# SBUF tiles that take their buffers from lists, in a two-layer graph transformer on one core

## The chip, the core and the metric

The kernel runs on one core of a Trainium2 chip. The core has TensorE (PE, matrix products into PSUM), VectorE (DVE), ScalarE (ACT), GpSimd (POOL) and SyncE (SP); DMAs move data between HBM and the on-chip memory SBUF, or within SBUF. The engines run side by side, each through its own instructions in a fixed order, and wait for each other by semaphores. The metric is the device time of one execution in microseconds (us), the median of several runs.

## What is computed

32 graphs of 512 nodes with 256 features, each with its own 512 x 512 adjacency matrix, go through two layers; a residual and a layer norm close each of them. Cut to what matters:

```python
# layer 0
allowed = (adj > 0) | (adj.T > 0) | eye
q, k, v = split(x @ Wqkv.T + bqkv)               # 8 heads of 32
attn = softmax(where(allowed, q @ k.T / sqrt(32), -inf))
h = layernorm(x + (attn @ v) @ Wo.T + bo) * g1 + b1_
h = layernorm(h + relu(h @ W1.T + b1) @ W2.T + b2) * g2 + b2_
x = layernorm(x + h)
# layer 1: attention alone, with the mask adj != 0
x = layernorm(x + attention(x, adj) @ Wo.T + bo)
```

Everything is in float32 but the masks, which are bfloat16.

## The kernel before

A class `Graph` holds the tiles of one graph and one small method for each step. Of a layer's attention, the part that matters here works on chunks of 128 keys x 4 heads x 512 queries; a layer has 8 of them, k = 0 to 7, of which 0 to 3 belong to the first four heads. For chunk k of a layer:

- `scores` (L404): 8 products on TensorE in narrow tiles write s, which takes 4 of the 8 PSUM banks. There is only one s, so the next `scores` waits until `exp` has read it.
- `exp` (L413): ScalarE writes p = exp(scale * s), 128 x 2048 float32, 1.88 us.
- `masked` (L417): VectorE multiplies p by the mask in place.
- `product` (L424): TensorE multiplies p with v into acc.
- For the softmax's sums, the four p of a head group are added up. `pair(layer, k)` (L437) is a DMA issued by GpSimd that adds p(k + 1) into p(k) within SBUF, 1 MB; `fold` (L440) adds two p on VectorE; `halve` (L464) adds one half of a p's partitions into the other by a DMA, and `spread` (L469) takes four pieces of it to a tile `part`. Where the sums aren't spread, `sums` (L448) adds over the keys with a product by ones.

So some p are last read by TensorE or VectorE, and others (1 and 5 of each layer, above all) by a DMA that lands some microseconds after it is issued.

The order of all this is written out by hand: `opening` for the first graphs (called with graphs 0 to 4 as a to e), `period` for the steady part (called 26 times; graphs k to k + 4 are at different stages of their way), `closing` for the last five (graphs 27 to 31 as a to e). The block runs under a manual schedule: each engine gets its instructions in the order in which the lines are written. A method only names its engine. `bias`, `masks`, `join` and the norms of five graphs thus lie between the products of others.

Tiles come from pools. `at(tag, n, shape)` asks a pool for a tile with a tag. The tag has a fixed number of buffers: 8 for p, 4 for y, r and st, 2 for z, v, kT and total. In the kernel before, the pool gives out one of these buffers by itself. The tile then waits for every user of the tile that had the buffer before: `exp` into a p waits until the old p's last reader is done, be it an engine or a DMA. PSUM banks for all products but s and acc don't go this way: `bank` takes the number of the bank from a string, `banks`, one digit for each tile in the order of asking, with a pattern repeated 13 times (for two calls of `period` each) between an opening and a closing part.

The places that the prediction speaks of, in the order of the code: in `opening`, graph 0's `pair(0, 4)` at L688 and graph 1's `exp(0, 3)` at L698; further down

```python
            a.exp(1, 5)          # L955
            ...
            a.exp(1, 6)          # L970
            ...
            a.pair(1, 4)         # L1013
            ...
            c.scores(0, 2)       # L1026
            c.exp(0, 2)          # L1027
            ...
            c.scores(0, 1)       # L1034
            ...
            c.exp(0, 5)          # L1041
```

and in `closing` `b.pair(1, 4)` (L1898), `d.exp(0, 1)` (L1922) and `d.exp(0, 4)` (L1935).

Of the kernel before, what the change touches and what calls it, by code (L numbers as in the profile page):

```python
# [9 lines left out]
F32 = mybir.dt.float32  # L10
# [17 lines left out]
def kernel(ctx: ExitStack, tc: tile.TileContext, t: dict, out: bass.AP):  # L28
# [14 lines left out]
    B, N, D = x.shape  # L43
    P = 128
    NQ = N // P
# [19 lines left out]
    total = const.tile([P, N // HD], F32, name="total")  # L65
# [85 lines left out]
    def plain(pools: ExitStack):  # L151
# [4 lines left out]
        ps_d = pools.enter_context(tc.tile_pool(name="ps_d", bufs=3, space=PSUM))  # L156
        hbm = pools.enter_context(tc.tile_pool(name="hbm", bufs=2, space=bass.MemoryType.DRAM))

        def dense(out, lhsT, rhs, start, stop, wide):
# [3 lines left out]

        SPREAD = {(0, 0), (1, 0)}

        banks = iter(
            "012012021021122121012012010210210210201012102021121021012012012012102102102102102020120122021201212101120120212010"
            + "120121212010121212012012120120021212102101010212101010210210102102201010" * 13
            + "102120201210021021010210102102102021201021010210202101201201210210212102102102121021021021021021202102120120"
        )  # L170

        SMALL = {"y", "z", "cent", "sT", "total", "r", "st", "part"} | {
            f"{t}{n}" for t in ("mv", "rs", "ms") for n in range(1, 5)
# [2 lines left out]
        class Graph:  # L176
# [6 lines left out]
            def at(self, tag, n, shape, dtype=F32, **kw):  # L183

                key = (tag, n)
                if key not in self.tiles:
                    name = f"{tag}_{self.b}" + "".join(f"_{i}" for i in (n if isinstance(n, tuple) else () if n is None else (n,)))
                    pool = small if tag in SMALL else ps_s if tag == "s" else ps_a if tag == "acc" else work
                    self.tiles[key] = pool.tile([P, *shape], dtype, tag=tag, name=name, **kw)
                return self.tiles[key]  # L190

            def bank(self, kind, n, shape):

                key = (kind, n)
                if key not in self.tiles:
                    name = f"ps{kind}_{self.b}" + "".join(f"_{i}" for i in n)
                    self.tiles[key] = ps_d.tile([P, *shape], F32, tag=f"d{next(banks)}", name=name, bufs=1)
                return self.tiles[key]

            def final(self, layer):  # L200

                return self.b == B - 1 and layer == 1


            @property
# [191 lines left out]
            def scores(self, layer, k):  # L397
                hg, kc = divmod(k, NQ)
                s = self.at("s", (layer, k), [HPC, N])
                for j in range(HPC):  # L400
                    at = slice(j * HD, (j + 1) * HD)
                    for half in range(2):
                        key = kc * P + half * P // 2
                        nc.tensor.matmul(  # L404
                            s[half * P // 2 : (half + 1) * P // 2, j, :],
                            self.kT(layer)[at, hg, key : key + P // 2],
                            self.qT(layer)[at, hg, :],
                            start=True,
                            stop=True,
                        )  # L410
# [31 lines left out]
            def sums(self, layer, hg):  # L442

                ps = self.bank("R", (layer, hg), [N])
                folded = [2 + hg] if not self.final(layer) else range(hg * NQ, (hg + 1) * NQ)
                for k in folded:
                    for j in range(HPC):
                        nc.tensor.matmul(  # L448
                            ps[j * HD : (j + 1) * HD, :],
                            ones,  # L450
                            self.p(layer, k)[:, j, :],
                            start=(k == folded[0]),
                            stop=(k == folded[-1]),
                        )


            def spread_out(self, layer, hg):

                return (layer, hg) in SPREAD and not self.final(layer)

            def halve(self, layer, hg, rows):

# [2235 lines left out]
    with ExitStack() as pools:  # L2698
        plain(pools)
# [207 lines left out]
```

## Time and profile before

| | |
|---|---|
| time before, median of 3 runs | 3014.59 us (3012.68 to 3015.29) |
| the profiled execution's own time | 3012.29 us |
| its span, first to last instruction | 3010.5 us |
| granted TensorE clock, mean | 0.995 |
| `exp` L413, ACT | 512 times, 1881 ns each, 963.0 us busy |
| `masked` L417, DVE | 512 times, 2278 ns each, 1162.5 us busy |
| `fold` L440, DVE | 189 times, 2281 ns each, 431.0 us busy |
| `pair` L437, DMA | 189 times, 1024 KB, 7.9 us from issue to landing (median) |
| share of DMA engines in use | 0.6 to 0.7 in most slices |

A row of busy times gives an engine, its busy time, its share of the span and its number of instructions. In the slices, each digit is the busy share of a fortieth of the span in tenths. A line of the list of waits says who waited, at which line, for what, and then the total in us, the number of times and the longest. A line of the timeline has start, length, engine, line, operation, tile written and tiles read; in brackets it has the idle time of the engine before it and what ended it. A line of the stretches has the stretch, its length, the busy time of PE, PEld, DVE, ACT and POOL with the number of instructions, the granted clock (1.00 is full), the share of the DMA engines and GB/s. The idle time of an engine that nobody waits for costs nothing.

### The profile page before, as it was taken

Reading aid. Unit: us, or ns where it says so; the run is one execution under the profiler, and the core shown is the slowest. Engines: PE = TensorE matmul, PEld = TensorE weight load, DVE = VectorE, ACT = ScalarE, POOL = GpSimd, SP = SyncE. Lnnn points to the kernel's source line nnn. Section 1 sums busy time; section 2 is a strip of 40 time slices with the busy share of each in tenths; the row PEclk is TensorE's granted clock in tenths of the full one; section 3 lists DMA queues with packets and bytes.
Section 4 is the critical chain, followed back from the end, with each engine's and each line's share of the span. In section 5 each row is a group of like instructions: output and inputs, shape, how many; then the busy total and the mean of one; then the engine's idle time right before and its main releaser. Section 6 shows DMA issues by size and latency. Waiting matters only on the chain.

```text
span 3010.5 us, 82999 instructions
## 1 busy us (share of the span) xinstructions
PE 2959.1 (98%) x36442; PEld 1375.9 (46%) x36442; DVE 2707.0 (90%) x3588; ACT 1746.2 (58%) x2111; POOL 972.2 (32%) x1252
## 2 busy tenths in 40 slices
PE   7989999999999999999999999999999999999997
PEld 2544445544444444445444445444454444454443
DVE  4879999999999999999999999999999999998996
ACT  4446655566565566565566655665655665556654
POOL 0222433233333233333233332333332333323241
PEclk9999999999999999999999999999999999999999
DMA  7867767676666676676666666766666776767560
GB/s 157 137 118 134 140 130 138 128 144 126 135 136 126 129 146 134 131 137 125 137 135 135 132 132 127 147 127 132 134 130 130 145 132 128 137 127 136 102 113 27
DMA packets 277169, 391.22 MB, mean 130 GB/s; under 512 B 153376, under 2 KB 237472, under 8 KB 246048
## 3 DMA queue, kind: packets, MB, share of 16 engines
q0 software_dynamic: 36304, 264.53, 47.6%
q1 hardware_dynamic: 240496, 121.32, 18.4%
q8 instruction: 288, 4.72, 0.7%
q14 instruction: 81, 0.66, 0.1%
HBM read 72.23 MB, written 33.55 MB: 35 GB/s over the span
## 4 chain that ended last, share of the span: by engine, by line
PE 93%; DVE 3%; DMA 2%; ACT 1%; issue 1%; POOL 1%; SPq 0%; DVEq 0%; POOLq 0%; ACTq 0%
PE s L404 17%; PE psF L162 14%; PE acc L424 14%; PE psH L162 14%; PE psQK_None L162 11%; PE psV L162 7%; PE psO L162 7%; PE psQK L162 4%; PE psT L365 2%; PE psR L448 2%; DMA p<-p 1%; DVE p L417 1%; ACT p L413 1%; DVE p L440 1%; DMA w_L_gnn_Wqkv<-in_L_gnn_Wqkv_dram 0%
## 5 line engine op out<-in xcount | busy, mean ns | idle before, releaser
L413 ACT ACTIVATE p<-s 128x2048 f32<-128x2048 f32 x512 | 963.0, 1881 | 496.2 <-PE s L404 459.8
L417 DVE TENSOR_TENSOR p<-p,m 128x2048 f32<-128x2048 f32 x512 | 1162.5, 2278 | 49.9 <-ACT p L413 46.7
L404 PE MATMUL s<-qT,kT 32*64 32x512 f32 x8192 | 572.7, 615 | 22.7 <-ACT p L413 21.4
L424 PE MATMUL acc<-p,v 128*32 128x512 f32 x4096 | 507.7, 596 | 1.6 <-ACT cT L433 1.5
L162 PE MATMUL psH<-xT,w_L_gnn_W 128*32 128x256 f32 (+1 forms) x6200 | 471.2, 380 | 1.5 <-DVE bov L321 1.5
L162 PE MATMUL psF<-w_L_gnn_W,hT 128*32 128x256 f32 (+1 forms) x6704 | 459.9, 380 | 0.0
L440 DVE TENSOR_TENSOR p<-p,p 128x2048 f32<-128x2048 f32 x189 | 431.0, 2281 | 10.7 <-DMA p<-p 9.4
L539 POOL TENSOR_SCALAR rs<-mv 128x2 f32<-128x2 f32 (+1 forms) x320 | 196.5, 614 | 726.6 <-DVE mv L534 713.3
L162 PEld LDWEIGHTS psH<-xT,w_L_gnn_W 128*32 128x32 f32 (+1 forms) x6200 | 302.7, 119 | 199.1 <-issue 55.3
L540 POOL TENSOR_TENSOR rs<-rs,neg_half 128x2 f32<-128x2 f32 (+1 forms) x320 | 369.7, 1155 | 26.7
L162 PEld LDWEIGHTS psF<-w_L_gnn_W,hT 128*32 128x32 f32 (+1 forms) x6704 | 291.2, 116 | 178.8 <-ACT hT L575 32.6
L437 POOL DMA_DIRECT2D p<-p x189 | 174.1, 921 | 530.0 <-PE acc L424 460.4
L575 ACT ACTIVATE hT<-psH,c_L_gnn_b 128x256 f32<-128x256 f32 x512 | 211.4, 474 | 200.0 <-PE psH L162 200.0
L404 PEld LDWEIGHTS s<-qT,kT 32*64 32x64 f32 x8192 | 119.5, 130 | 335.4 <-issue 113.2
L464 POOL DMA_DIRECT2D p<-p x126 | 107.8, 855 | 464.5 <-DVE mv L534 196.2
L162 PE MATMUL psQK_None<-xT,w_L_gnn_Wqkv 128*32 128x512 f32 (+1 forms) x2012 | 246.5, 598 | 5.6 <-DMA w_L_gnn_Wqkv<-in_L_gnn_Wqkv_dram 4.7
L162 PE MATMUL psO<-w_L_gnn_Wo,cT 128*32 128x256 f32 (+1 forms) x2776 | 241.8, 381 | 1.8 <-DVE cT L510 1.8
L424 PEld LDWEIGHTS acc<-p,v 128*32 128x32 f32 x4096 | 119.7, 110 | 253.0 <-issue 187.9
L162 PEld LDWEIGHTS psO<-w_L_gnn_Wo,cT 128*32 128x32 f32 (+1 forms) x2776 | 155.3, 123 | 99.2 <-issue 45.6
L370 ACT COPY xT<-psT 128x512 f32<-128x512 f32 x130 | 76.0, 585 | 198.9 <-PE psT L365 198.8
L560 ACT ACTIVATE x<-z,ms,rs 128x256 f32<-128x256 f32 x128 | 73.2, 597 | 167.2 <-DVE ms L544 164.0
L531 DVE BATCH_NORM_STATS2 st<-y 128x6 f32<-128x256 f32 x384 | 155.0, 422 | 6.2
(77 smaller groups left out, 2845.3 us busy)
## 6 DMA issues: line engine op xcount, KB each, us to landing
p<-p POOLq DMA_DIRECT2D x189, 1024.0 KB, 7.9
p<-p POOLq DMA_DIRECT2D x63, 512.0 KB, 5.9
x<-in_x_dram SPq DMA_DIRECT2D x32, 512.0 KB, 4.2
code<-in_adj_dram POOLq DMA_DIRECT2D x32, 512.0 KB, 5.9
m<-code SPq DMA_DIRECT2D x32, 512.0 KB, 4.9
out_dram<-x SPq DMA_DIRECT2D x32, 512.0 KB, 6.2
p<-p POOLq DMA_DIRECT2D x63, 256.0 KB, 6.3
part<-p SPq DMA_DIRECT2D x252, 64.0 KB, 2.0
```

The costliest lines, as they stand in the source:

```text
L162: nc.tensor.matmul(out[at], lhsT[:, at], rhs, start=start, stop=stop)
L404: nc.tensor.matmul(s[half * P // 2 : (half + 1) * P // 2, j, :], self.kT(layer)[at, hg, key : key + P // 2], self.qT(layer)[at, hg, :], st ...
L413: nc.scalar.activation(self.p(layer, k), self.at("s", (layer, k), [HPC, N]), AF.Exp, scale=SCALE)
L417: nc.vector.tensor_tensor(p, p, m[:, k % NQ, None, :].to_broadcast([P, HPC, N]), ALU.mult)
L424: nc.tensor.matmul(acc[j * HD : (j + 1) * HD, :], self.v(layer)[:, kc, h * HD : (h + 1) * HD], self.p(layer, k)[:, j, :], start=(kc == 0), ...
L437: nc.gpsimd.dma_start(out=self.p(layer, k), in_=self.p(layer, k + 1), accum_op=ALU.add)
L440: nc.vector.tensor_tensor(self.p(layer, dst), self.p(layer, a), self.p(layer, b), ALU.add)
L464: nc.gpsimd.dma_start(out=p[:rows], in_=p[rows : 2 * rows], accum_op=ALU.add)
L531: nc.vector.bn_stats(self.at("st", (n, i), [6]), self.y(n, i))
L539: nc.gpsimd.tensor_scalar(rs, self.mv(n)[:, a:b, 1:2], EPS, None, ALU.add)
L540: nc.gpsimd.tensor_tensor(rs, rs, neg_half[:, a:b, None], ALU.pow)
L575: nc.scalar.activation(self.hT(h)[:, f, :], ps[:, f % 2, :], AF.Relu, bias=b1[:, f : f + 1])
```

## The change

Eight kinds of tile in SBUF (p, y, z, st, r, v, kT and total) take their buffer from a string of digits, as the PSUM banks did and do. In `at`, a tag found in `slots` is replaced by the tag with the next digit, with one buffer of its own. The number of buffers of each kind stays the same, and so does the order of the steps. `final` is renamed `direct`, with the same meaning.

```diff
-        banks = iter(
-            "012012021021122121012012010210210210201012102021121021012012012012102102102102102020120122021201212101120120212010"
...
-        )
+        slots = {
+            "d": iter(
+                "012012021021122121012012010210210210201012102021121021012012012012102102102102102020120122021201212101120120212010"
...
+            ),
+            "p": iter(
+                "012345673267415013405762302764517064153205732146706431520752136450436217051726431"
+                + "036472501257436206435710271536470436152075216435036421705172436106437250125736420436571027156437036415207521436506432170517236410436725012576432036457102715436706431520752136450436217051726431" * 2
+                + "03642750175246370435612072516437063124563452170"
+            ),
+            "y": iter(
+                "01231023012301231023100113201320232301321023020231201302"
+                + "303021031230232301321023020231201302" * 8
+                + "3202132031200210203102312020021032101230"
+            ),
+            "z": iter(
...
+            "st": iter(
...
+            "r": iter(
...
+            "v": iter(
+                "0110011"
+                + "0011" * 13
+                + "00110"
+            ),
+            "kT": iter(
...
+            "total": iter(
...
+        }
...
                     pool = small if tag in SMALL else ps_s if tag == "s" else ps_a if tag == "acc" else work
+                    if tag in slots:
+                        tag, kw = f"{tag}_{next(slots[tag])}", {"bufs": 1}
                     self.tiles[key] = pool.tile([P, *shape], dtype, tag=tag, name=name, **kw)
...
-                    self.tiles[key] = ps_d.tile([P, *shape], F32, tag=f"d{next(banks)}", name=name, bufs=1)
+                    self.tiles[key] = ps_d.tile([P, *shape], F32, tag=f"d_{next(slots['d'])}", name=name, bufs=1)
...
-            def final(self, layer):
-
-                return self.b == B - 1 and layer == 1
+            def direct(self, layer):
+
+                return (self.b, layer) == (B - 1, 1)
```

## The prediction

> **What bounds the kernel now.** I read four views in this order: the page's busy times, its slices, the list of TensorE's waits, and the timeline around the longest of those waits. First busy times and slices:
>
> ```profile
> PE 2959.1 (98%) x36442; PEld 1375.9 (46%) x36442; DVE 2707.0 (90%) x3588; ACT 1746.2 (58%) x2111; POOL 972.2 (32%) x1252
> PE   7989999999999999999999999999999999999997
> ```
>
> TensorE has 3010.5 - 2959.1 = 51.4 us without a matmul, and the slices put it at both ends: the middle is full. The steady part shows this best, cut into stretches of one repetition (91.58 us, PE busy next to it):
>
> ```profile
> 450.00:541.58 91.58, 91.58 (x1120) 43.02 (x1116) 84.71 (x113) 54.56 (x67) 30.85 (x39) 1.00 0.68 134
> 2000.00:2091.58 91.58, 91.58 (x1124) 43.03 (x1116) 84.71 (x113) 54.56 (x66) 31.29 (x39) 1.00 0.68 133
> ```
>
> There TensorE never waits, so no choice of buffers can shorten the 26 repetitions; it can only spoil them. A gain must come from the 51.4 us at the ends. What they wait for, in TensorE's own list of waits (us in total, times, longest):
>
> ```profile
> PE s L404 <- ACT p L413: 21.4, 19, 8.5
> PE psT L365 <- DMA x<-in_x_dram: 4.9, 1, 4.9
> ```
>
> and, from the view of line 413, what the exponentials themselves waited for (us, times):
>
> ```profile
>   PE s L404: 459.8, 349
>   DMA p<-p: 16.7, 3
> ```
>
> Three exponentials waited for a DMA that moves p into p. An exponential reads scores s and writes a fresh p; such a DMA gives it no data. It can only have been waiting for its buffer, which the DMA was still reading. The timeline shows the largest of the three, and below it the chain of waits gives the transfer's length:
>
> ```profile
> 178.91 1.11 PE L404 MATMUL s<-qT,kT 32*64 32x512 f32 x16
> 179.96 3.66 PE L162 MATMUL psF<-w_L_gnn_W,hT 128*32 128x256 f32 x64
> 180.65 1.08 POOL L437 DMA_DIRECT2D p<-p  x1
> 190.18 1.88 ACT L413 ACTIVATE p<-s 128x2048 f32<-128x2048 f32 x1 [11.34 <-DMA p<-p]
> 192.09 2.29 DVE L417 TENSOR_TENSOR p<-p,m 128x2048 f32<-128x2048 f32 x1 [8.54 <-ACT p L413]
> 192.11 2.02 PE L404 MATMUL s<-qT,kT 32*64 32x512 f32 x16 [8.49 <-ACT p L413]
> ...
> 180.65 9.45 DMA p<-p
> ```
>
> The scores end at 180.02; the exponential starts at 190.18, just after the transfer lands (180.65 + 9.45 = 190.10). All of s's PSUM is held meanwhile, so TensorE stops at 183.62, and VectorE with it. The two others are at 68.77 (1.05 us) and 2755.20 (4.29 us).
>
> **What the Trainium skill says.** "Perfetto Trace Analysis", Optimization Strategy, takes *consistent* bubbles on the engine that should be saturated as a hint that buffers are too few. Here the bubbles are three single ones and the repetitions have none, so the number of buffers (8) suffices, and which one is taken is what hurts. "TensorE: Matmul & The Clock Gate", What's actually happening, says that about 3.4 us of idling halves the clock until a busy window has passed. The trace agrees, in stretches with the granted clock third from the end:
>
> ```profile
> 188.00:192.00 4.00, 0.00 (x0) 0.00 (x0) 0.00 (x0) 1.82 (x2) 0.00 (x0) 0.56 0.92 183
> 192.00:194.00 2.00, 1.89 (x16) 0.33 (x16) 1.91 (x1) 0.53 (x2) 0.00 (x0) 0.50 0.69 103
> 194.00:196.00 2.00, 2.00 (x17) 1.83 (x10) 0.72 (x2) 1.78 (x2) 0.00 (x0) 0.68 0.45 93
> ```
>
> So the stall is paid once more after it ends. "DMA: Bandwidth & Descriptors", Anatomy of one DMA, fits a GpSimd-issued DMA as 2.0 us + bytes / 436e3, which for this 1,024 KB gives 4.4 us; here the median is 7.9 us and these two took 9.45 and 10.83, so I use the trace's.
>
> **The change, part by part.**
>
> *Order.* Built, both programs have the same instructions in the same order on all five engines. TensorE's and SyncE's waits are the same too. What differs is addresses and, on ACT, DVE and POOL, waits for a buffer's last users. Following each tile to the tile that had its buffer before it: 279 of 512 p and 54 of 384 y follow another tile; st, r, z, v, kT and totals follow the same one as before, so those lists change nothing. The rename of `final` changes nothing either.
>
> *Waits added.* For every wait that only the changed program has, I looked up the instruction that ends it and when that ended in the trace of before. The tightest, once in each repetition, is an exponential (at 368.94, 460.51, ... 2658.39) that takes a p whose fold on VectorE ended 2.84 us before. Next come 3.28 us (exponential at 2758.40) and 5 us and up; VectorE's tightest is 5.2 us, POOL's 18. None binds: 0 us. ACT gains 28 semaphore instructions, median 38 ns in the view of line 413, 1.1 us over the run on an engine idle 42% of the time: 0 as cost, bound 0 to 1.1.
>
> *Waits removed that did bind.* Only three exponentials in the program lose a wait that ended within 0.5 us of their start. They are the three above.
>
> (1) 190.18, `c.exp(0, 2)`: it held the buffer of p(1, 5) of graph 0, which `a.pair(1, 4)` reads. The list gives it that of p(1, 6), whose last user, a fold, ended at 177.94. It then waits for its scores alone, so it starts at 180.1 and ends at 182.0, before TensorE runs out at 183.62. The 8.49 us go. VectorE finished at 183.55, so its 8.54 us go too, and both engines continue in the same relation as before. The clock: from 192.11 the three groups s x16, psT x4, psF x16 took until 198.67 (6.56 us); the same three took from 2761.77 to 2766.77 at full clock (5.00 us). So 1.56 us come back, at most; the matmuls after it that wait for VectorE had 2.16 us and more to spare. (1) is 8.49 + 1.56 = 10.05, bounds 8.49 and 10.05.
>
> What is late next: the buffer under the DMA now goes to `c.exp(0, 5)`, which started at 199.89. Moved by 10.05 it would start at 189.84, and the transfer lands at 190.10: 0.3 us late. Behind it on ACT is a relu (203.49) that had 1.72 us of idling before it, so nothing passes on. SyncE's loads in 184 to 203 don't move with TensorE; the nearest consumer is the transpose of `part` at 207.10, landed at 194.46, 12.6 us to spare against 10.05.
>
> (2) 2755.20, `d.exp(0, 1)` in the closing:
>
> ```profile
> 2755.20 1.88 ACT L413 ACTIVATE p<-s 128x2048 f32<-128x2048 f32 x1 [4.29 <-DMA p<-p]
> 2757.14 1.12 PE L404 MATMUL s<-qT,kT 32*64 32x512 f32 x16 [2.51 <-ACT p L413]
> ...
> 2744.29 10.83 DMA p<-p
> ```
>
> Its scores ended at 2751.99; the new buffer's fold at 2748.85. It starts at 2752.1, ends at 2753.9, and TensorE goes on at 2754.63: 2.51 us. The buffer under the DMA (landing 2755.12) goes to `d.exp(0, 4)`, which moves from 2758.40 to 2755.89: still 0.7 us to spare. No halved clock here. Bounds 1.8 and 2.51.
>
> (3) 68.77: the exponential could start at 67.88, 0.9 us earlier. But VectorE's fold at 68.75 needs the same transfer's data, and later an edge mask's load, paced by SyncE's queue, ends a wait of all:
>
> ```profile
> 89.81 1.22 DVE L284 TENSOR_TENSOR m<-m,m 128x2048 bf16<-128x2048 bf16 x1 [3.20 <-DMA m<-code]
> 92.50 3.72 PE L162 MATMUL psH<-xT,w_L_gnn_W 128*128 128x256 f32 x16 [1.54 <-DVE bov L321]
> ```
>
> That load doesn't come earlier, so I take 0, bounds 0 and 0.9.
>
> **Sum.** 10.05 + 2.51 + 0 = 12.56 us. Span 3010.5 - 12.6 = 2997.9; the profiled execution took 3012.29, 1.8 around its span, hence 2999.7. The median shown is 2.3 us above that execution, so 3014.59 - 12.56 = 3002.0. Least: 8.49 + 1.8 - 1.1 = 9.2, 3005.4. Most: 10.05 + 2.51 + 0.9 = 13.5, 3001.1.
>
> **The rivals.** A measurement of this kernel can tell about 0.2%, 6 us, from no change; so faster means under 3008.6.
>
> *The wait only moves on.* The same transfer stalls `c.exp(0, 5)` instead. For it: 0.3 us late already. Against: 1.72 us of idle ACT behind it. The longest p<-p landing in the trace is 11.9 us, 2.45 more than this one; then 2.75 - 1.72 = 1.0 us is lost, and the clock's 1.56 as well: 3002.0 + 2.6 = 3004.6.
>
> *VectorE takes it back.* It is busy 84.7 of 91.58 us in a repetition, and the stall was also its rest. Were it behind by then, TensorE would wait for it within a repetition and the 8.49 return. For it: 90% busy. Against: it stood idle through the same stall, with nothing queued. Then 2.51 + 1.56 = 4.1 are left: 3010.5, no change.
>
> *A new wait in every repetition.* The exponential with 2.84 us to spare is the place. Every us by which VectorE's fold comes later than that costs 1 us in each of 26 repetitions. To end 6 us above 3014.59, 18.6 us beyond the gain, it takes 0.72 us each: the fold 3.6 us later than now. For it: 26 times the leverage. Against: the spare time is 2.84 or 2.85 in all of them, with nothing moved inside a repetition. At that point: 3021.
>
> *The lists choose what the pool chose.* So it is for six of the eight kinds. For p it is excluded by the 279.
>
> **How the numbers follow.** Both stalls go, 0.74, 3002.0; the wait moves on, 0.13, 3004.6; VectorE takes it back, 0.08, 3010.5; a new wait, 0.05, 3021. Faster 0.87, same 0.08, slower 0.05. Predicted 3002.0. Range 2998.5 to 3007: the sums above (3001.1 to 3005.4) with some 2 us for the spread of the runs shown (3012.68 to 3015.29), holding the first two cases.
>
> **What would show it.** Right: no exponential with a wait for DMA p<-p; TensorE's longest wait on ACT p far under 8.5 us; granted clock 1.00 from 180 to 200; 91.58 us in the middle as before; the psH after the bov wait still at 92.5. Wrong: a wait over 0.5 us at `c.exp(0, 5)`, TensorE waiting for DVE p before 300 us, a repetition longer than 91.6, or a new bubble in the closing.

## The result, and the profile after

Run in turns on the same chip, six times each, the changed kernel took 2999.16 us (2997.37 to 2999.72) and the kernel before 3012.35 us (3011.72 to 3015.29): a ratio of 0.995, interval 0.994 to 0.9961. The forecast was 3002.0, 2.8 us more. The gain between the medians is 13.2 us, against 12.56 summed, and the interval, some 12 to 18 us, holds both. But 12.56 had been taken off 3014.59, the median of the first three of these six runs of before, and the median of all six is 3012.35. The profiled execution of the changed kernel took 2999.72 us.

The page after, in its span, busy times and the slices of TensorE:

```profile
span 2998.0 us, 83024 instructions
PE 2959.6 (99%) x36442; PEld 1374.8 (46%) x36442; DVE 2707.0 (90%) x3588; ACT 1747.1 (58%) x2111; POOL 978.6 (33%) x1252
PE   7999999999999999999999999999999999999997
```

TensorE is busy for as long as before (2959.1), in a span that is 12.5 us shorter: 38.4 us without a matmul are left of 51.4. The second slice, which was an 8, is a 9. The middle is unchanged, in the same two stretches of one repetition (length, then busy time and instructions of PE, PEld, DVE, ACT and POOL, granted clock, DMA share, GB/s), as are the ones around the first stall, which is gone:

```profile
450.00:541.58 91.58, 91.58 (x1127) 42.94 (x1116) 84.74 (x113) 54.57 (x66) 30.94 (x40) 1.00 0.70 134
2000.00:2091.58 91.58, 91.58 (x1118) 42.93 (x1117) 84.71 (x113) 54.56 (x67) 31.15 (x39) 1.00 0.68 133
...
184.00:188.00 4.00, 4.00 (x33) 2.88 (x22) 3.39 (x3) 2.35 (x2) 0.00 (x0) 1.00 0.96 195
188.00:192.00 4.00, 4.00 (x45) 1.52 (x47) 4.00 (x5) 0.00 (x0) 0.00 (x0) 1.00 1.08 152
192.00:194.00 2.00, 2.00 (x44) 1.19 (x39) 1.08 (x5) 1.43 (x1) 1.25 (x3) 1.00 0.73 153
```

From 188 to 192 us TensorE had done nothing before, at a granted clock of 0.56; now it is busy in all of it, at 1.00. TensorE's list of waits (us in total, times, longest) says the same, and the line of the exponentials says what they themselves still wait for (us, times):

```profile
PE s L448 <- ACT p L457: 9.5, 17, 2.0
PE psT L409 <- DMA x<-in_x_dram: 4.9, 1, 4.9
```

```profile
  PE s L448: 482.8, 359
  DMA p<-p: 5.2, 1
```

One exponential out of three still waits for a DMA of p. The timeline of 179 to 196 us shows which (start, length, what, and in brackets the idle time before it and what ended it):

```profile
179.16 1.11 PE L448 MATMUL s<-qT,kT 32*64 32x512 f32 x16
180.38 1.89 ACT L457 ACTIVATE p<-s 128x2048 f32<-128x2048 f32 x1 [1.29 <-PE s L448]
181.03 1.22 POOL L481 DMA_DIRECT2D p<-p  x1
...
188.89 1.11 PE L448 MATMUL s<-qT,kT 32*64 32x512 f32 x16
191.67 5.36 PE L162 MATMUL psH<-xT,w_L_gnn_W 128*32 128x256 f32 x96
192.57 1.88 ACT L457 ACTIVATE p<-s 128x2048 f32<-128x2048 f32 x1 [5.20 <-DMA p<-p]
194.35 0.83 ACT L619 ACTIVATE hT<-psH,c_L_gnn_b 128x256 f32<-128x256 f32 x2
```

`c.exp(0, 2)` now starts at 180.38, as soon as its scores are there. The transfer issued at 181.03 holds the buffer of `c.exp(0, 5)`, which starts at 192.57. That is the wait that moved on. No bracket stands behind the TensorE lines: its next scores come at 200.41, after acc, psH and psR products that need nothing of this exponential.

To see where the time went, take the same TensorE instruction in both traces and subtract its start before from its start after. The columns are places in the order of the work, named by their time in the trace of before; the rows below the first belong to the experiments, told further down:

```
                      183.00  192.11  199.15  2752.94  2757.14  2769.09  2983.79
changed kernel         +0.25   -8.31   -9.78    -9.65   -12.23   -12.23   -12.57
p as the pool chose    -0.41   -0.47   -0.36    -0.33    -0.35    -0.35    -0.35
only at 190            -0.85   -9.41  -10.88   -10.41   -10.43   -10.43   -10.78
only at 2755           -0.94   -0.82   -0.82    -0.68    -3.26    -3.26    -3.25
ten tiles              -1.51  -10.08  -11.54   -10.98   -13.56   -13.56   -13.90
only at 68             +0.62   +0.64   +2.05    +1.98    +1.99    +3.41    +3.41
```

In the changed kernel 8.56 us are gained at the first stall (183.00 to 192.11), 1.47 in the matmuls after it (to 199.15), 2.58 at the one in the closing, and 0.34 late in the closing, at a product (2955.17 in the trace of before) whose wait for VectorE fell from 0.59 to 0.24 us; why it fell I didn't follow. All 26 repetitions, between 199.15 and 2752.94, move it by 0.13. The first column is the opening: it differs from execution to execution, by -1.51 to +2.15 us in the thirteen traces of this document, also between executions of one kernel, so the steps from one column to the next tell more than the last column.

### The profile page after: what moved, and what is told of

Same layout as the page of the kernel before. It is cut to its first block, busy times and chain, and to the rows that moved or that the text cites. A ratio compares the mean times of both kernels' runs of the same rounds, so it can differ in the third digit from the quotient of the medians.

```text
span 2998.0 us, 83024 instructions
## 1 busy us (share of the span) xinstructions
PE 2959.6 (99%) x36442; PEld 1374.8 (46%) x36442; DVE 2707.0 (90%) x3588; ACT 1747.1 (58%) x2111; POOL 978.6 (33%) x1252
## 4 chain that ended last, share of the span: by engine, by line
PE 95%; DVE 2%; DMA 1%; ACT 1%; POOL 0%; issue 0%; SPq 0%; DVEq 0%; POOLq 0%; ACTq 0%
PE s L448 17%; PE psH L162 15%; PE psF L162 15%; PE acc L468 15%; PE psQK_None L162 11%; PE psO L162 7%; PE psV L162 7%; PE psQK L162 4%; PE psT L409 2%; PE psR L492 2%; DVE p L461 1%; ACT p L457 1%; DVE p L484 1%; DMA p<-p 1%; DMA w_L_gnn_Wqkv<-in_L_gnn_Wqkv_dram 0%; PE psB L354 0%
```

## The experiments

The lists of digits say little to the eye, so each edit is given as what it changes: which tile took the buffer of which earlier tile, with p(layer, k) as in the methods. All later digits of the list follow from that and keep every other succession. One of them in full, to show what such an edit looks like in the code (the last of four lines of the list, the third experiment against the first):

```diff
-                + "07126534730452610721465375036142071234657605423107215346740631520712653473045261072146537035641237452610731025643754201654160237"
+                + "07126534730452610721465375036142071234657605423107215346740631520712653473045261072146537053641257432610751023645734201634160257"
```

The first four ran together, each beside the kernel before (3013.84 us, median of 35).

**The other lists without p.** The changed kernel, with p alone put back to the buffers that the pool had chosen, all else as changed:

```diff
-279 p follow another tile in their buffer than before
+every p follows the tile that it followed before
```

> The changed kernel, but p's list gives each p the buffer whose last tile it followed in the kernel before; the other seven lists stay. Theory (only p's choice counts): as before, 3012 to 3015 us, ratio 1.000 +- 0.001, with the stalls of 8.5 us near 190 us and 2.5 us near 2755 us back. Rival (addresses, one-buffer tags, or y's list bring part of the gain): ratio 0.999 or less.

3012.91 us, ratio 0.9998 (0.9989 to 1.0006). TensorE's wait is back in its old size:

```profile
PE s L449 <- ACT p L458: 21.7, 20, 8.4
```

In the trace the kernel ends 0.35 us under before, all of it from the opening (-0.41 at 183.00). So the other lists, y's 54 new successions and the rename bring nothing; the time is in the list of p.

**The first stall alone.** Against the first experiment:

```diff
-graph 2: p(0, 2) after p(1, 5), p(0, 1) after p(1, 6), p(0, 5) after p(1, 7), all of graph 0
+graph 2: p(0, 2) after p(1, 6), p(0, 1) after p(1, 7), p(0, 5) after p(1, 5), all of graph 0
```

> As the run before, but the three p around 190 us (chunks 2, 1 and 5 of graph 2's first layer) take the buffers of the changed kernel. Theory: 10.0 us faster than before (8.49 of stall and up to 1.56 of clock), ratio 0.9967; granted clock 1.00 from 180 to 200 us; the stall near 2755 us stays. Rival (the wait only moves to chunk 5): 2.6 us less gain, 7.4 us. Rival (VectorE takes it back): under 4 us.

3003.13 us, ratio 0.9968 (0.996 to 0.9976), 10.7 us under the kernel before.

```profile
PE s L449 <- ACT p L458: 13.0, 18, 3.0
```

**The stall in the closing alone.** The edit in full is above; in tiles:

```diff
-graph 30: p(0, 1) after p(1, 5), p(0, 4) after p(1, 6), both of graph 28
+graph 30: p(0, 1) after p(1, 6), p(0, 4) after p(1, 5), both of graph 28
```

> As the first of these runs, but only the two p around 2755 us (chunks 1 and 4 of graph 30's first layer) take the buffers of the changed kernel. Theory: 2.5 us faster than before, ratio 0.9992; the stall of 8.5 us near 190 us stays. Rival (a later step of the closing takes it back): ratio 1.000.

3010.93 us, ratio 0.999 (0.9982 to 0.9998), 2.9 us less. The long wait at 190 stays in the list:

```profile
PE s L449 <- ACT p L458: 18.6, 18, 8.6
```

**Ten tiles and nothing else.** The kernel before, with one list for p that changes ten tiles: the five of these two places and five of graph 1 at the wait of 68 us. `y`, `r` and all other kinds stay in their pools.

```diff
+        p_slots = iter(
...
                 if key not in self.tiles:
...
+                    if tag == "p":
+                        tag, kw = f"p_{next(p_slots)}", {"bufs": 1}
```

> The kernel before with one list, for p alone: each p follows the tile that it followed before, but ten p at the three places (five near 68 us, three near 190, two near 2755) take the buffers of the changed kernel. Theory: the whole gain of the change, ratio 0.995 to 0.996. Rival (the other 269 p, or y, bring a part): gain under 11 us.

3000.12 us, ratio 0.9955 (0.9942 to 0.9968), 13.7 us less; the two parts above make 10.7 + 2.9 = 13.6. The line of waits is, but for the line numbers, that of the changed kernel:

```profile
PE s L413 <- ACT p L422: 9.5, 17, 2.0
```

The sums of medians agree better than their intervals of some 2 to 4 us to either side allow one to expect. The traces are sharper: from 183.00 to the last column this kernel gains 12.39 us and the changed kernel 12.82. Ten of 512 tiles are the whole change, within half a us. The other successions that it alters are neither gain nor loss beyond that.

The next four ran together too (the kernel before: 3013.88 us, median of 33).

**The held buffer goes to the very next exponential.** This is the rival of the wait that only moves on, made to happen: of the changed kernel's p two are swapped, so that the transfer in flight holds `c.exp(0, 1)` instead of `c.exp(0, 5)`.

```diff
-graph 2: p(0, 1) after p(1, 7), p(0, 5) after p(1, 5), both of graph 0
+graph 2: p(0, 1) after p(1, 5), p(0, 5) after p(1, 7), both of graph 0
```

> The changed kernel, but near 190 us the buffer under the transfer goes to the very next exponential (chunk 1 of graph 2's first layer) and not to the one after it (chunk 5). In the changed kernel's trace that exponential starts at 185.02 and the scores after it at 188.89, and the transfer landed near 192.5. Theory (a late buffer costs what it keeps the scores waiting): the exponential ends at 194.4, the scores and TensorE stop for 3.5 to 5.5 us, gain falls to 8 to 10 us, ratio to before 0.997. Rival (only the exponential that meets the transfer first matters, or TensorE has other work): as the changed kernel, 0.9955.

3008.43 us, the median of 21 runs that scatter from 3002.87 to 3017.29; ratio 0.9982 (0.9973 to 0.999). The gain left is 5.5 us, where 8 to 10 were expected. This timeline is of its profiled execution, which took 3012.97:

```profile
187.23 3.62 PE L162 MATMUL psF<-w_L_gnn_W,hT 128*128 128x256 f32 x16
193.58 1.88 ACT L458 ACTIVATE p<-s 128x2048 f32<-128x2048 f32 x1 [8.95 <-DMA p<-p]
195.51 1.87 PE L449 MATMUL s<-qT,kT 32*64 32x512 f32 x16 [4.66 <-ACT p L458]
...
223.33 1.01 PE L410 MATMUL psT<-ident,x 128*128 128x128 f32 x4 [2.87 <-ACT p L458]
```

The stall returns at 4.66 us, of the size expected, because nothing stands behind these scores that can do without the exponential. Against the same TensorE instructions in the trace of the changed kernel, this execution loses 4.73 us at the stall and 1.65 in the matmuls after it. These 6.4 us are what the buffer costs here.

It loses 2.93 us more at the psT of 223.33 and 1.46 in the matmuls after that, and this wait is a different one. The bracket of the last line shouldn't be believed: the exponential named there ended at 222.45, 0.9 us earlier, and in the changed kernel the same psT starts at 212.13, ahead of its exponential (212.30). TensorE's weight loads show that it had come as far as the first psT at 220.40, and that the next load then waited for nothing that the profile shows:

```profile
220.40 0.14 PEld L410 LDWEIGHTS psT<-ident,x 128*128 128x128 f32 x1 [0.81 <-issue]
223.33 0.60 PEld L410 LDWEIGHTS psT<-ident,x 128*128 128x128 f32 x3 [2.80 <-issue]
```

The DMA packets of the traces name a likely cause, the instructions themselves. A queue of its own (q8 on the page of a profile) moves 288 packets of 16 KB, one for every 254 of TensorE's 73,240 matmuls, weight loads and waits. Each of them comes within 77 instructions of the same place in TensorE's order in every trace, but for one packet of this execution. In the twelve other traces that packet comes when TensorE has begun 4321 to 4385 instructions; here it comes at 4545, when TensorE has just stopped. It moves from 221.00 to 221.93, and the work goes on at 223.33. So TensorE had most likely run out of instructions; that the edit led to it was not tried, and why the packet was late stays open. The same stretch has a second late transfer: p into p, 1 MB, issued at 206.51, took 17.1 us, where it took 8.9 to 10.5 in the twelve others.

How many of the 21 runs had such a wait no trace tells; the wide scatter may come from it. By the buffer's 6.4 us alone a run would take some 3004.4 (an estimate, from 2997.98 for the changed kernel run beside it), and the five fastest took 3002.87 to 3005.28. The median stands 10.5 us over the changed kernel's, close to the 10.77 that the four losses of the trace make, but that is chance: the profiled execution took 4.5 us more than the median, and its opening was 1.9 us later than the changed kernel's.

That a wait 8.95 us long before the very next exponential takes TensorE's time again is clear without all this.

**The wait at 68 us alone.** Against the first experiment:

```diff
-graph 1: p(0, 3) after p(0, 5), p(0, 7) after p(0, 2), p(0, 5) after p(0, 4), p(0, 1) after p(0, 6), p(0, 4) after p(0, 7), of graph 0
+graph 1: p(0, 3) after p(0, 6), p(0, 7) after p(0, 7), p(0, 5) after p(0, 5), p(0, 1) after p(0, 2), p(0, 4) after p(0, 4), of graph 0
```

> p as the pool chose it, but the five p near 68 us take the buffers of the changed kernel. Theory: 0, ratio 1.000 +- 0.001, the exponential there starts 0.9 us earlier and the edge mask's load still sets when the products at 92 us start. Rival (it brings what the sum lacks): 1 to 2 us, ratio 0.9995.

3012.15 us, ratio 0.9996 (0.9988 to 1.0005): nothing, as forecast. Its trace served for something else. In the closing it has the old stall, and a clock that before had not shown there (the granted clock is the third number from the end):

```profile
2755.00:2759.00 4.00, 1.60 (x24) 0.44 (x16) 3.27 (x4) 1.80 (x2) 0.00 (x0) 0.97 0.67 99
2759.00:2763.00 4.00, 3.88 (x44) 1.37 (x48) 2.29 (x1) 3.29 (x6) 0.00 (x0) 0.60 0.87 238
```

**A fold a little too late, in every repetition.** This is the rival of the new wait. In 25 repetitions the exponential whose buffer comes from a fold gets that of a fold 1.70 us later than the spare time allows:

```diff
-graph g: p(1, 3) after p(0, 6), p(1, 5) after p(0, 4), both of graph g + 1
+graph g: p(1, 3) after p(0, 4), p(1, 5) after p(0, 6), both of graph g + 1
```

> The changed kernel, but in 25 of the 26 repetitions two p exchange their buffers: chunk 3 of the second layer takes one whose fold on VectorE ends 1.70 us after this exponential's start in the changed kernel, chunk 5 one that is long free. Theory: the scores after it have some 0.5 us to spare, so TensorE stops 1.2 us in each repetition: 25 x 1.2 = 30 us, near 3029 us, ratio to before 1.005. Rival (the repetition has room, the engines shift against each other and the wait vanishes): as the changed kernel.

3030.55 us, ratio 1.0065 (1.005 to 1.0081). TensorE waits 25 more times (42 for 17), and the repetition has a hole:

```profile
PE s L449 <- ACT p L458: 38.7, 42, 2.0
```

```profile
450.00:541.58 91.58, 90.38 (x1112) 42.09 (x1113) 83.38 (x111) 53.46 (x64) 29.67 (x38) 1.00 0.68 133
```

In 91.58 us TensorE is busy for 90.38. From 278 to 2753 us it falls 31.8 us behind the changed kernel's pace, 1.27 in each of the 25; some 30 were expected. So the lists can lose as well as gain, and far more where a repetition is hit.

**The changed kernel once more**, to see it beside the same runs of before:

> The changed kernel once more, for the size of its gain beside the others: the sum of the stalls says 12.5 us, ratio 0.9958; the first runs gave 0.995 with an interval of 0.994 to 0.9961.

2997.98 us (2997.2 to 2999.53), ratio 0.995 (0.9937 to 0.9964): 15.9 us under the 3013.88 of these runs.

**A kernel with both stalls, three executions more.** The kernel of the first experiment, unedited, one profiled execution each, to show how much an execution with the stalls varies, and where.

> The first of these kernels once more (p as the pool chose it), with a profile, for the price of the stalls in clock. Theory: the two stalls are 8.4 to 8.6 and 2.5 us in every execution, and what differs is the stretch at half clock after them: 6.8 or 10.2 us near 190, none or 3.4 us near 2757, and the time goes with it (near 3012 with the shortest, near 3015 with the longest). Rival (the spread comes from the opening alone): the same stretches near 190 and 2757 in all.

> As the run before, a second execution of the same kernel: theory and rival expect the same as there, each with its own stretches.

> As the two runs before, a third execution of the same kernel: theory and rival expect the same as there, each with its own stretches.

3012.46, 3015.01 and 3013.57 us. These are the stretches after the first stall, in the first of them

```profile
192.00:196.00 4.00, 3.76 (x24) 2.02 (x25) 2.63 (x2) 2.31 (x3) 0.00 (x0) 0.56 0.50 102
196.00:200.00 4.00, 4.00 (x34) 2.57 (x36) 3.34 (x5) 0.71 (x2) 0.00 (x0) 1.00 0.28 81
```

and in the second:

```profile
192.00:196.00 4.00, 1.87 (x16) 0.34 (x16) 1.89 (x1) 2.35 (x2) 0.00 (x0) 0.50 0.71 145
196.00:200.00 4.00, 4.00 (x22) 3.44 (x15) 2.58 (x3) 2.35 (x2) 0.00 (x0) 0.65 0.31 74
```

In the first the clock is whole again at 196 us, in the second it is still at 0.65. Part of that is a stall 2.0 us later in the run; the rest is a longer halved stretch. The two executions with the longer stretch took longer, as the theory had it, but the rival has its part: at the end of the table's row the second stands 2.73 us over before and the third 1.29, and 2.04 and 0.37 of that are from the opening. From the traces with both stalls or one of them, the length of the halved clock (granted 0.5) at each, and what the matmuls behind the first stall lost (before: the 1.47 us of the table; the others by their own shift from 183.00 to 199.15, added to it):

```
                       at the first stall     lost     at the stall in the closing
before                       6.8 us          1.47 us          none
p as the pool chose          6.8             1.52             none
once more, 1                 6.8             1.54             none
once more, 2                10.2             2.21             none
once more, 3                10.2             2.39             none
only at 68                  10.2             2.90             3.4 us, 1.42 us lost
only at 2755                 6.8             1.59             (no stall)
only at 190                (no stall)         -               none
```

So the same stall is worth up to 1.4 us more in some executions at the first place, and as much again in the closing. (A part of the lost time can be in the stall itself: in the third execution it was 0.17 us longer.)

The same traces show what decides. The granted clock changes only at steps of 3.413 us, and all changes of one trace lie on one grid (in before, from 21.197 to 188.450 us are 49.0 steps), which lies at another place in every trace. At the first stall, where the step in which TensorE sets to work again held 3.17 to 3.40 us of matmuls, the halving ended with that step and had lasted 6.8 us (four traces); where it held 1.27 to 2.61, one step more was halved (three traces). In the closing, the emptiest step at the stall held 1.25 us of matmuls in the one trace that was halved after it, and 1.55 to 1.97 in the six that weren't. So one and the same stall has several prices, by where it happens to lie on the grid.

## Why the prediction was right, and where it was not

**The mechanism, part by part.** The sum was made against the profiled execution and came out at 2999.7; the changed kernel's profiled execution took 2999.72. Term by term: 10.05 at the first place, 10.03 measured (8.56 of stall and 1.47 of clock, for 8.49 and 1.56); 2.51 in the closing, 2.58 measured; 0 at 68 us, 0 measured alone. What was not in the sum is small: +0.25 up to 183.00 and the 0.34 late in the closing. That the two totals agree to 0.02 us is luck, as the opening alone differs by 3.7 us between traces; that the terms agree to 0.1 is not. The psH after the bov wait, which I wanted "still at 92.5", came 0.42 later. Nothing says that this is the change's doing: that place lies between -1.34 and +2.21 us in the eleven experiments, and the second of the three executions more, which has every p where the pool put it, is the +2.21.

**The term that failed** is the last line of the sum: "The median shown is 2.3 us above that execution, so 3014.59 - 12.56 = 3002.0". It took the distance between a profiled execution and a median of three runs for a fixed amount and carried it over to the changed kernel. Measured, it is 0.06 us for before, with three runs more (3012.35 and 3012.29), and -0.56 us for the changed kernel (2999.16 and 2999.72). So 2.24 us of the 2.8 by which the forecast was too high are three runs taken for the kernel, and the other 0.6 are the gain itself, 13.2 for 12.56, which is within its interval.

It depends much on which execution was profiled. The 35 and 33 runs of before beside the experiments have medians of 3013.84 and 3013.88, 1.6 us above that same execution. Of the kernels without either stall, the ten tiles' median stands 1.72 us over its profiled execution, which had the earliest opening of all (-1.51 us), and the changed kernel's, run again, 1.55 under. Two things are seen to differ between executions with the stalls. One is the opening, which differs as much without them. The other is the clock after the stalls, which the change takes away. I had priced that clock from one execution, at 1.56 us and "No halved clock here", and gave "at most" with it. It is 1.5 to 2.9 us at the first stall and 0 to 1.4 at the second. The Trainium skill, "TensorE: Matmul & The Clock Gate", What's actually happening, gives a window of 3413 ns and calls it free-running; the grids of 3.413 us, each at its own place, agree with it, and the halved stretches after these stalls are 3.4, 6.8 and 10.2 us long, one, two or three of them. An execution that pays the high price stands higher before and gains more, so "at most" was wrong.

The runs without a profile fit this without proving it: in those beside the first four experiments, the kernel before took 3012.9 us in the mean of 16 with a granted clock of 0.995 and 3014.0 in 15 with 0.994 (the other four, with less, took 3014.7 to 3025.8). The changed kernel, run again, had 0.996 or 0.997 in all five. Those clocks hold the opening and the end of the run too.

By the traces the gain is 13.0 us (10.03 + 2.58 + 0.34) against an execution of before that pays the low price, and (0.05 + 0.07 + 0.74 + 0.92 + 1.43 + 1.42) / 6 = 0.8 us more against the mean of the six that have both stalls (before, p as the pool chose, the three executions more, only at 68): 13.7. The medians gave 13.2, 13.7 (ten tiles) and 15.9, and 13.7 lies within the interval of each of them. For the 2 us by which the last one stands above it there is no trace; they stay open.

**What is late next** was right in its place and wrong in its size. I put the transfer's end at 190.10 and the wait of `c.exp(0, 5)` at 0.3 us. The transfer landed 2.4 us later than that, and the exponential started 2.46 us after the 190.11 to which TensorE had moved it (199.89 - 9.78). So the relu behind it, with 1.72 us to spare, was passed 0.64 us (194.35 for 203.49 - 9.78). "Nothing passes on" was wrong for ACT. It was right for TensorE, which didn't need that relu so soon: the second relu is on time again (197.10 for 206.88 - 9.78). My sign for being wrong, "a wait over 0.5 us at `c.exp(0, 5)`", came, and no time was lost with it. It asked for idle time on an engine that isn't the bottleneck; the sign should have been a wait of TensorE on that exponential. The transfer was mis-sized for a reason that repeats: it took 9.40 to 9.57 us in all seven traces in which TensorE stands still for it, and 11.16 to 11.59 in the five in which TensorE goes on. Its length was read from a trace with the stall in it, and used for a kernel without.

**The rivals.** *The wait only moves on* had the lateness nearly right (2.75 us, 2.46 measured) and the price not: 1.0 us on TensorE and 1.56 of clock, where it was 0. The fifth experiment shows that this was a matter of which exponential gets the buffer; given to the next one, it cost 6.4 us in that trace. *VectorE takes it back* fell: it goes on with TensorE, and neither the clock nor a wait for it shows up to 300 us. *A new wait in every repetition* was not in the change (91.58 and 91.58 again), but its leverage is real: 1.27 us, 25 times. *The lists choose what the pool chose* fell for p, and holds in effect for all of it but ten tiles.

The other steps held: waits added cost nothing (the 26 exponentials with 2.84 us to spare still have it to spare in the trace of the changed kernel), and so did the semaphore instructions that ACT gained.

## What to carry to other kernels

Where a bubble is single and its repetitions have none, don't ask for more buffers; ask which buffer the late instruction got, who reads it last, and which later instruction can best bear that wait. Then price the stall from several executions, not one: what a stall leaves behind in the clock varied here by 1.4 us, nearly as much as the 1.56 that was put in for it. Don't carry the distance between a profiled execution and a median of few runs over to the changed kernel; the 2.3 us of three runs were 0.06 with six. The length of a transfer, too, can depend on the stall that it causes. And look for the wait that moves on by whether the bottleneck waits for it, not by whether something does.

## What the runs showed of the hardware

- The same stall of about 8.5 us was followed by 6.8 us of halved clock in four of seven traces and by 10.2 in three. In the closing a stall of 2.5 us was followed by none in six and by 3.4 us in one.
- The granted clock changed on a grid of 3.413 us. In these stalls a step of full clock with 1.25 us of matmuls or less was followed by a halved one, and one with 1.55 or more was not; a halved step with 2.61 us or less was followed by another, and one with 3.06 or more was the last. Where between these figures the limits lie the traces don't show.
- The transfer of 1 MB of p into p landed after 9.40 to 9.57 us where TensorE and VectorE stood still for it, and after 11.16 to 11.59 where both went on (in the changed kernel with a DMA share of 1.08 from 188 to 192 us, for 0.92 before). That the work beside it is the cause was not tried.
- Each wait of TensorE over 2.8 us in the fifth experiment was followed by slower matmuls that lost about another 1.5 us (1.65 after 4.66 us, 1.46 after 2.87), as much as the 8.5 us stall of before with its 1.47. A short stall near this length can so cost a third to a half as much again.
- In one trace a 16 KB packet of what are most likely TensorE's instructions came 200 instructions later than usual, and TensorE stood for 2.87 us.
